# A residual block with shared and routed experts in fp32: second-stage sums kept in PSUM over a block, both first-stage matrices in one bank, a last unit by tokens

## The chip, the core and the metric

The kernel runs on one core of one Trainium2 chip, in fp32 throughout. The metric is the device time of one execution in microseconds (us). The engines are TensorE (PE, matmuls), VectorE (DVE), ScalarE (ACT), GpSimd (POOL, here the indirect gathers and scatters) and SyncE (SP, which issues most DMAs). Matmul results lie in PSUM, in eight banks of 128 partitions x 512 fp32 numbers.

## What is computed

x has 4 x 1024 tokens of 512 numbers; N = 4096 tokens in all. Two layers follow each other, each with a residual:

```python
ys = cond / sqrt(512);  d = rsqrt((ys * ys) @ (w0 * w0) + eps)
x1 = x + ((x * ys) @ w0) * d                          # layer 0
shared = (silu(x1 @ w1) * (x1 @ w3)) @ w2             # 512 -> 1024 -> 512
s = sigmoid(concat(x1, cond) @ router_W)              # 8 experts
# the two best by s + bias; their gates are s, divided by the sum of both
routed = sum of gate_e * (gelu(x1 @ W1e[e]) @ W2e[e]) # 512 -> 512 -> 512, exact gelu
out = x1 + (shared + routed) / 3
```

## The kernel before, in words

**Blocks, units, slots.** The tokens are cut into NB = 8 blocks of TB = 512. A block's shared expert is done in HU = 4 units (class Shared, L719); unit u takes two 128-wide chunks of the hidden width and all 512 tokens. A routed expert is done in slots (class Slot, L953): 256 gathered rows that belong to one expert. SURE = 32 slots are always there; as many more as the routing needs (two here) run in a tc.Switch on the register `spare` (L1207).

**Order of the work.** Layer 0 for all blocks (to about 140 us); Shared units of blocks 0 to 5 (to 578 us); slots 0 to 31 (to 998); the Switch with slots 32 and 33 (to 1038); Shared units of blocks 6 and 7, "the late units". In the late units DVE also adds the routed rows to the tokens (gather_picks and add_picks, L1082 to L1109), in portions that `pump()` hands out at fixed points. Before them the base rows of blocks 0 to 5 are stored to DRAM, and come back as `sum` for this addition.

**Seven products.** Nearly every matrix product is done on 2 x 2 quarters with seven products and sums of quarters (the Winograd form). LO and HI are the first and the last 256 columns. In a Shared unit the *first stage* computes x1 @ w1 (matrix i = 0, the gate) and x1 @ w3 (i = 1, the value). Product n of matrix i is four instructions of 256 columns. Products 1, 6, 5, 3 add up in one chain, whose value between them is copied out by ACT (evict, L773 to L776); 2, 7 and 4 are added to those copies by DVE (add, L778 to L780). Products 6, 5 and 3 need sums of weights, which weight_sums (L418 to L427) makes on DVE for the units of block 0, one unit ahead, a task for each matrix; and sums of tokens (token_sums, L402 to L412).

The *second stage* of a unit, h @ w2, runs one unit later: `rest(prev, task)` (L782) weaves four parts of the unit before (seconds, L846) between its own products. A part's products go to three PSUM banks, a chain and two others (sa, sb, sc in the profile), and its drain (L871 to L881) multiplies by 1/3 and adds to the block's base rows on DVE, seven times a unit. hidden_sums (L830 to L837) makes the sums of h that the second stage needs. Block 0 uses plain matmuls there (plain, L890), with 512 columns and four banks that add up over the block. After the block's last unit `store` writes the base rows out.

**PSUM.** Two pools, bank_a and bank_b, of four banks each in rotation (L95 to L99). A unit takes four bank_a tiles: chain and other, each for both matrices, with half of `chain` unused.

**Order set by hand.** `tasks` (L1151 to L1175) maps a half unit to the small works done at its end: fetches of expert weights on SP's queue (fetch_first, L916, four DMAs of 256 KB from W1e; fetch_second, L922, one of 1 MB from W2e), the router's steps (sigmoid, picks, counting), the sums. In a slot, `rest` issues fetch_first(j + 3) (L996) and, while it runs the parts of the slot before, fetch_second of that slot's j + 3 (L1074). All these fetches stand in SP's queue in the order in which they are issued, among the stores and loads of base rows; ACT's queue carries the stores of the slots' results (ys_d). The main loop is L1204 to L1231.

Of the kernel before, what the change touches and what calls it, by code (L numbers as in the profile page):

```python
# [25 lines left out]
FP = mybir.dt.float32  # L26
# [18 lines left out]
def kernel(  # L45
# [46 lines left out]
    ps_a = ctx.enter_context(tc.tile_pool(name="ps_a", bufs=4, space=bass.MemoryType.PSUM))  # L92
    ps_b = ctx.enter_context(tc.tile_pool(name="ps_b", bufs=4, space=bass.MemoryType.PSUM))

    def bank_a(name):  # L95
        return ps_a.tile([P, TB], FP, tag="a", name=name)

    def bank_b(name):
        return ps_b.tile([P, TB], FP, tag="b", name=name)  # L99

# [407 lines left out]
    def open_pools():  # L508
        lin_ctx.close()
        later["row"] = ctx.enter_context(tc.tile_pool(name="row", bufs=6))  # L510
        sums = ctx.enter_context(tc.tile_pool(name="sums", bufs=1))
        hs = sums.tile([P, 3 * TH], FP, name="hs")
        more = sums.tile([P, 3 * TH], FP, name="more")
        later["hs"] = [hs[:, ts(n, TH)] for n in range(3)]
        later["more"] = [more[:, ts(n, TH)] for n in range(3)] + [falling.rearrange("p t e -> p (t e)")]
        work = ctx.enter_context(tc.tile_pool(name="work", bufs=1))
        t_tiles.append(work.tile([P, 3 * KH * TH], FP, name="t1"))
        later["g"] = work.tile([P, 2 * TB], FP, name="g")
        later["h"] = [work.tile([P, 2 * TB], FP, name=f"h{i}") for i in range(2)]
        rt = rt_ctx.enter_context(tc.tile_pool(name="rt", bufs=1))  # L520
        for name in ("sel", "hit", "one", "two"):
            later[name] = rt.tile([P, NT, E], FP, name=name)
        for name in ("picked", "run"):
            later[name] = rt.tile([P, E, NT], FP, name=name)
        for name in ("top", "den", "live", "half"):
            later[name] = rt.tile([P, NT], FP, name=name)
        for name in ("cnt", "shift", "ns", "upto"):
            later[name] = rt.tile([P, E], FP, name=name)
        later["last"] = rt.tile([P, E + 1], FP, name="last")
        later["full"] = rt.tile([P, E, N // GS], FP, name="full")  # L530
        later["edge"] = rt.tile([P, N // GS], FP, name="edge")
        later["own"] = rt.tile([P, NSLOT, E], FP, name="own")
        later["ownf"] = rt.tile([P, NSLOT], FP, name="ownf")
        later["high"] = [rt.tile([P, NT], I32, name=f"high{i}") for i in range(2)]
        later["low"] = [rt.tile([P, NT], I32, name=f"low{i}") for i in range(2)]
        later["addr"] = addr
        later["toks_raw"] = toks_raw
# [181 lines left out]
    class Shared:  # L719


        py = {}

        def __init__(self, blk, u):
            self.blk, self.u = blk, u
            self.seven = False

        def product(self, out, i, n, start):
# [19 lines left out]
            for k in range(KH):  # L748
# [7 lines left out]
                )  # L756

        def begin(self):

            blk, u = self.blk, self.u  # L760
            self.chain = [bank_a(f"ch{i}_{blk}_{u}") for i in range(2)]
            self.other = [bank_a(f"ot{i}_{blk}_{u}") for i in range(2)]
            for i in range(2):
                self.product(self.chain[i][:, LO], i, 1, True)
            for i in range(2):
                self.product(self.other[i][:, LO], i, 2, True)

        def sevens(self):
            for i in range(2):
                self.product(self.other[i][:, HI], i, 7, True)  # L770
            self.seven = True

        def evict(self, m, cols):  # L773

            for c, p in zip(self.c, self.chain):
                nc.scalar.activation(c[:, m, cols], p[:, LO], AF.Copy)  # L776

        def add(self, half, m, cols):  # L778
            for c, p in zip(self.c, self.other):
                nc.vector.tensor_tensor(c[:, m, cols], p[:, half], c[:, m, cols], ALU.add)  # L780

        def rest(self, prev, task):  # L782
            g, h = self.c = [t.rearrange("p (m t) -> p m t", m=2) for t in (later["g"], later["h"][self.at % 2])]
            self.h = h
            none = (lambda: None, lambda: None)
            parts = prev.parts() if prev is not None else [none] * 4
            self.evict(0, LO)
            for i in range(2):
                self.product(self.chain[i][:, LO], i, 6, False)
                if not self.seven:  # L790
                    self.product(self.other[i][:, HI], i, 7, True)
            self.add(LO, 0, LO)
            pump()
# [3 lines left out]
            drain()  # L797
            for i in range(2):
                self.product(self.chain[i][:, LO], i, 5, False)
            self.evict(1, HI)  # L800
            mm, drain = parts[1]
            mm()
            self.add(HI, 1, HI)
            drain()
            pump()
            for i in range(2):
                self.product(self.chain[i][:, LO], i, 3, False)
            nc.scalar.activation(g[:, 0, HI], self.chain[0][:, LO], AF.Silu)
            nc.scalar.activation(g[:, 0, LO], g[:, 0, LO], AF.Silu)
            mm, drain = parts[2]  # L810
            mm()
            nc.vector.tensor_tensor(h[:, 0, HI], g[:, 0, HI], self.chain[1][:, LO], ALU.mult)
            nc.vector.tensor_tensor(h[:, 0, LO], g[:, 0, LO], h[:, 0, LO], ALU.mult)
            drain()
            task(2 * self.at)
            pump()
            for i in range(2):
                self.product(self.other[i][:, HI], i, 4, False)
            mm, drain = parts[3]
            mm()  # L820
            self.add(HI, 1, LO)
            nc.scalar.activation(g[:, 1, :], g[:, 1, :], AF.Silu)
            drain()
            nc.vector.tensor_tensor(h[:, 1, :], g[:, 1, :], h[:, 1, :], ALU.mult)
            if self.blk > 0:
                self.hidden_sums()
# [18 lines left out]

        def seconds(self, part):  # L846
            blk, u, h = self.blk, self.u, self.h
            if part == 0:
                self.bank2 = [bank_b(f"s{n}_{blk}_{u}").rearrange("p (s d) -> p s d", s=2) for n in "abc"]
            chain, two, seven = self.bank2  # L850
            a11, a12, a21, a22 = h[:, 0, LO], h[:, 1, LO], h[:, 0, HI], h[:, 1, HI]
# [3 lines left out]
            for out, a, b, start in (  # L855
                [(chain, a11, b1[:, LO], True), (two, a12, b2[:, LO], True)],
                [(seven, a21, b1[:, HI], True), (chain, s2, t2, False)],
                [(chain, s1, t1, False)],
                [(chain, s4, b2[:, HI], False), (seven, a22, t4, False)],
            )[part]:  # L860
# [10 lines left out]
        def drain(self, part):  # L871
            blk = self.blk
            chain, two, seven = self.bank2
            for bank, m, half in (
                [(chain, 0, LO), (two, 0, LO)],
                [(seven, 1, HI), (chain, 1, LO)],
                [(chain, 1, HI)],
                [(chain, 0, HI), (seven, 1, LO)],
            )[part]:
                r = base[blk][m][:, :, half]  # L880
                nc.vector.scalar_tensor_tensor(r, bank, third, r, ALU.mult, ALU.add)  # L881
            if part == 3 and self.u == HU - 1:
                self.store()

        def store(self):
# [4 lines left out]
        def plain(self, m):  # L890
            blk, u = self.blk, self.u
            hc = 2 * u + m
            if hc == 0:
                self.py[blk] = [bank_b(f"ps{blk}_{s}") for s in range(NS)]
            for s in range(NS):
# [57 lines left out]
    class Slot:  # L953
# [26 lines left out]
        def rest(self, prev, task):  # L980
# [14 lines left out]
            parts[3]()  # L995
            if self.j + 3 < self.end:  # L996
                fetch_first(self.j + 3)
# [69 lines left out]
        def part3(self):  # L1067
# [5 lines left out]
            nc.scalar.dma_start(out=as_pair(ys_d, j * GS), in_=self.pair)  # L1073
            if j + 3 < self.end:  # L1074
                fetch_second(j + 3)
# [46 lines left out]
    def reload_last():  # L1122
        load_segments(nc.sync, later["segs"][:, : TB // Q, :], x1_d[ts(last_blk, TB)])

    def spare_pair(i):
        return later["segs"].rearrange("p q c -> p (q c)")[:, ts(i, 2 * D)].rearrange("p (s d) -> p s d", s=2)
# [24 lines left out]
    for u, work in (  # L1151
# [12 lines left out]
        (10 * HU + 4, [lambda: turn_rows(0)]),  # L1164
        (2 * early * HU, [lambda: fetch_second(1), lambda: fetch_second(2)]),
        (2 * late, [reload_last, lambda: out_sums(0, big[5])]),
        (2 * late + 1, [lambda: out_sums(1, big[5])]),
        (2 * late + 3, [lambda: out_sums(2, big[5])]),
        (2 * late + 2, [turn_last]),
        (2 * late + 5, [lambda: token_sums(last_blk)]),  # L1170
    ):
        tasks[u] += work
# [32 lines left out]
    for u, unit in enumerate(units):  # L1205
        if u == late:
            for n in tc.Switch(later["spare"], E):  # L1207
                prev.end = SURE + n
                last = prev
                for j in range(SURE, SURE + n):  # L1210
                    slot = Slot(j)
# [16 lines left out]
        prev = unit  # L1228
    for mm, drain in prev.parts():
        mm()  # L1230
        drain()  # L1231

# [38 lines left out]
```

## Time and profile before

| | us |
|---|---|
| median of 4 runs | 1197.2 (1196.25 to 1200.44) |
| the profiled execution | 1200.9 |
| its span | 1199.1 |
| layer 0 | 0 to 139.8 |
| Shared blocks 0 to 5 | 139.8 to 577.9 |
| slots 0 to 31 | 577.9 to 997.8 |
| Switch, slots 32 and 33 | 997.8 to 1037.6 |
| Shared blocks 6 and 7, end | 1037.6 to 1199.1 |

A profile's line names the line of the kernel, the engine, the operation, output and inputs by the program's names, the shape, and in brackets the idle time before it with what ended it. In the first stage `ch` is a chain bank and `ot` the other one; in a slot `ph` is the first stage, `yc` and `yo` the second. Matmul durations overlap a little: four instructions are listed with 1.03 us, but the next four begin 0.86 later.

The page's rows of the evictions and drains that the change touches, with count, busy time, mean ns of one and the idle time before them:

```profile
L776 ACT ACTIVATE g<-ch 128x256 f32<-128x256 f32 x96 | 36.7, 382 | 203.3 <-PE ch L749 191.5
L780 DVE TENSOR_TENSOR g<-ot,g 128x256 f32<-128x256 f32 x96 | 40.3, 420 | 56.8 <-PE ot L749 37.3
L881 DVE SCALAR_TENSOR_TENSOR base<-sa,base 128x512 f32<-128x512 f32 x88 | 60.7, 690 | 19.8 <-PE sa L862 18.9
...
L978 ACT ACTIVATE h<-ph 128x512 f32<-128x512 f32 x68 | 40.6, 597 | 156.3 <-PE ph L970 156.3
```

The first two have a twin for h; the third has some with other outputs. The last is a slot's eviction, with twice the columns of the first.

### The profile page before, as it was taken

Reading aid. Unit: us, or ns where it says so; the run is one execution under the profiler, and the core shown is the slowest. Engines: PE = TensorE matmul, PEld = TensorE weight load, DVE = VectorE, ACT = ScalarE, POOL = GpSimd, SP = SyncE. Lnnn points to the kernel's source line nnn. Section 1 sums busy time; section 2 is a strip of 40 time slices with the busy share of each in tenths; the row PEclk is TensorE's granted clock in tenths of the full one; section 3 lists DMA queues with packets and bytes.
Section 4 is the critical chain, followed back from the end, with each engine's and each line's share of the span. In section 5 each row is a group of like instructions: output and inputs, shape, how many; then the busy total and the mean of one; then the engine's idle time right before and its main releaser. Section 6 shows DMA issues by size and latency. Waiting matters only on the chain.

```text
span 1199.1 us, 15347 instructions
## 1 busy us (share of the span) xinstructions
PE 1169.2 (98%) x5138; PEld 957.9 (80%) x5138; DVE 710.9 (59%) x1569; ACT 224.7 (19%) x515; POOL 449.3 (37%) x448
## 2 busy tenths in 40 slices
PE   8999999999999999999989999999999998999997
PEld 5444576788888888888878888888888887787886
DVE  4547555666565655655644554554555554389897
ACT  2000031111221221211111222212212211221120
POOL 3000000344430112202356666676666760056640
PEclk9999999999999999999999999999999999999999
DMA  9599410210502016140297898888988885487861
GB/s 170 106 223 206 92 50 1 84 23 1 71 1 76 27 36 184 53 123 17 81 264 226 236 262 229 239 254 235 246 255 242 235 252 160 117 266 246 298 211 71
DMA packets 120153, 184.97 MB, mean 154 GB/s; under 512 B 13797, under 2 KB 48741, under 8 KB 120057
## 3 DMA queue, kind: packets, MB, share of 16 engines
q1 hardware_dynamic: 85944, 123.92, 39.7%
q0 software_dynamic: 16448, 35.26, 10.4%
q10 hardware_dynamic: 17664, 24.65, 6.3%
q8 instruction: 43, 0.70, 0.3%
q14 instruction: 54, 0.43, 0.2%
HBM read 139.14 MB, written 44.64 MB: 153 GB/s over the span
## 4 chain that ended last, share of the span: by engine, by line
PE 85%; DVE 6%; DMA 5%; issue 2%; SPq 1%; ACTq 0%; ACT 0%; DVEq 0%
PE ph L970 19%; PE ch L749 16%; PE ot L749 12%; PE yc L1028 10%; PE yo L1028 7%; PE sa L862 7%; PE pl L443 6%; PE sc L862 3%; PE ps L896 2%; DMA seg<-in_x_dram 2%; PE sb L862 2%; DMA big<-in_L_cond_W2e_dram 1%; DVE sum L1107 1%; DVE xsegs L881 1%; SPq L122 1%
## 5 line engine op out<-in xcount | busy, mean ns | idle before, releaser
L939 POOL DMA_INDIRECT xsegs<-x_d,toks x280 | 306.4, 1094 | 320.0 <-DVE xg L951 79.0
L654 POOL DMA_INDIRECT tok_d<-token,addr x64 | 64.7, 1010 | 287.2 <-DVE addr L644 272.2
L1041 DVE TENSOR_TENSOR yr<-yo,yr 128x256 f32<-128x256 f32 x102 | 43.3, 425 | 187.1 <-ACT yr L1038 95.3
L970 PE MATMUL ph<-xg,big 128*128 128x256 f32 x544 | 130.2, 383 | 4.7 <-DMA big<-in_L_cond_W2e_dram 4.7
L970 PE MATMUL ph<-t,big 128*128 128x256 f32 x544 | 128.5, 379 | 0.0
L443 PE MATMUL pl<-xT,wm 128*128 128x512 f32 (+1 forms) x288 | 117.4, 554 | 3.5 <-DVE xT L282 1.5
L970 PEld LDWEIGHTS ph<-xg,big 128*128 128x128 f32 x544 | 104.4, 192 | 19.5 <-issue 5.0
L970 PEld LDWEIGHTS ph<-t,big 128*128 128x128 f32 x544 | 103.4, 190 | 14.1
L749 PE MATMUL ot<-big,w_sb 128*128 128x256 f32 x448 | 110.4, 379 | 0.1
L1096 POOL DMA_INDIRECT big<-ys_d,addr x64 | 68.7, 1074 | 101.8 <-DMA xsegs<-x_d 56.7
L443 PEld LDWEIGHTS pl<-xT,wm 128*128 128x128 f32 x288 | 52.4, 190 | 55.3 <-issue 46.3
L749 PEld LDWEIGHTS ot<-big,w_sb 128*128 128x128 f32 x448 | 85.0, 190 | 12.8 <-issue 0.8
L1038 ACT ACTIVATE yr<-yc 128x256 f32<-128x256 f32 x136 | 52.1, 383 | 210.4 <-PE yc L1028 201.9
L776 ACT ACTIVATE g<-ch 128x256 f32<-128x256 f32 x96 | 36.7, 382 | 203.3 <-PE ch L749 191.5
L780 DVE TENSOR_TENSOR g<-ot,g 128x256 f32<-128x256 f32 x96 | 40.3, 420 | 56.8 <-PE ot L749 37.3
L881 DVE SCALAR_TENSOR_TENSOR base<-sa,base 128x512 f32<-128x512 f32 x88 | 60.7, 690 | 19.8 <-PE sa L862 18.9
L780 DVE TENSOR_TENSOR h<-ot,h 128x256 f32<-128x256 f32 x96 | 40.5, 422 | 50.7 <-PE ot L749 38.9
L1028 PE MATMUL yc<-w0t,g 128*128 128x256 f32 x272 | 69.9, 379 | 0.5 <-ACT yr L1038 0.5
L978 ACT ACTIVATE h<-ph 128x512 f32<-128x512 f32 x68 | 40.6, 597 | 156.3 <-PE ph L970 156.3
L749 PE MATMUL ch<-w0t,seg 128*128 128x256 f32 x256 | 62.6, 380 | 2.5 <-issue 2.5
L749 PE MATMUL ch<-t,seg 128*128 128x256 f32 x256 | 63.1, 379 | 0.0
L1028 PEld LDWEIGHTS yc<-w0t,g 128*128 128x128 f32 x272 | 51.6, 190 | 7.8 <-ACT yr L1038 0.9
(222 smaller groups left out, 1882.4 us busy)
## 6 DMA issues: line engine op xcount, KB each, us to landing
big<-in_L_cond_W1e_dram SPq DMA_DIRECT2D x140, 256.0 KB, 5.4
big<-in_L_cond_W2e_dram SPq DMA_DIRECT2D x34, 1024.0 KB, 7.8
ys_d<-yr ACTq DMA_DIRECT2D x34, 512.0 KB, 8.7
x_d<-back SPq DMA_DIRECT2D x32, 256.0 KB, 5.0
base<-x_d SPq DMA_DIRECT2D x13, 512.0 KB, 4.5
base_d<-base SPq DMA_DIRECT2D x12, 512.0 KB, 4.3
sum<-base_d SPq DMA_DIRECT2D x12, 512.0 KB, 7.1
out_dram<-sum SPq DMA_DIRECT2D x12, 512.0 KB, 4.5
```

Of the source, the lines that this page charges most:

```text
L443: nc.tensor.matmul(pas[oc][:, ds(lo, n)], lhsT=wms[b][:, k, oc, :], rhs=xTs[blk][:, k, ds(lo, n)], start=(k == 0), stop=(k == KC - 1),)
L654: ins = nc.gpsimd.indirect_dma_start(out=tok_d, out_offset=bass.IndirectOffsetOnAxis(ap=later["addr"][i][:, t : t + 1].bitcast(U32), axis= ...
L749: nc.tensor.matmul(out, lhsT=lhs[:, k, :], rhs=rhs[:, k, :], start=start and k == 0, stop=k == KH - 1, skip_group_check=not start,)
L780: nc.vector.tensor_tensor(c[:, m, cols], p[:, half], c[:, m, cols], ALU.add)
L862: nc.tensor.matmul(out[:, s], lhsT=a[:, ts(s, P)], rhs=b, start=start and s == 0, stop=True, skip_group_check=not (start and s == 0),)
L881: nc.vector.scalar_tensor_tensor(r, bank, third, r, ALU.mult, ALU.add)
L939: nc.gpsimd.indirect_dma_start(out=seg[:, q, :], out_offset=None, in_=x1_segs, in_offset=bass.IndirectOffsetOnAxis(ap=toks[:, c : c + 1].b ...
L970: nc.tensor.matmul(self.ph[:, i], lhsT=weights[j][0][:, k, ts(c, P)], rhs=xg[j][:, k, :], start=(k == 0), stop=(k == KC - 1),)
L1028: nc.tensor.matmul(out, lhsT=a[:, k, :], rhs=b[:, k, :], start=start and k == 0, stop=k == HC // 2 - 1, skip_group_check=not start,)
L1038: nc.scalar.activation(self.r[r][:, cols], self.chain[:, LO], AF.Copy)
L1041: nc.vector.tensor_tensor(self.r[r][:, cols], self.other[:, half], self.r[r][:, cols], ALU.add)
L1096: nc.gpsimd.indirect_dma_start(out=picks[t][i], out_offset=None, in_=ys_d, in_offset=bass.IndirectOffsetOnAxis(ap=at.bitcast(U32), axis=0) ...
```

## The change

1. *Second stage.* bank_b has four fixed banks b0 to b3. The products `two`, `seven` and a new `four` add up in b0 to b2 over all units of a block, and are drained only in the unit that `closes` it (u = 3; in block 7 u = 2). The chain has b3 in every unit. Drains go from seven a unit to four, and eight in the closing one.
2. *First stage.* Both matrices share banks: chain, `two` and `seven`, each with two halves of 256 columns, one for each matrix; three bank_a tiles a unit and not four. ACT evicts both halves in one instruction, into g and h that lie beside each other in one tile (hgh = h, g, h), and DVE adds both in one. As h takes turns on the two sides of g, the order of the matrices is (1, 0) in even units and (0, 1) in odd ones. In unit 0 of block 0, whose sevens are there already, the order of products stays; elsewhere both matrices' 6 come before both 7.
3. *Last unit* (block 7, u = 3). Its second stage is done by tokens (finish): eight plain matmuls of 512 columns into four banks, each drained and stored by itself (256 KB, SP and ACT in turn). It needs no hidden sums, but the unchanged half of w2's chunk 6, which a new task reloads (128 KB).
4. *Fetches.* fetch_second(1) is issued one task earlier, at the end of the last unit of block 5, and so ahead of slot 0's fetch_first(3) and the base stores in SP's queue. fetch_first(34) and fetch_second(33) are no longer issued before the Switch but inside its cases, where the case has such a slot. With two spare slots only fetch_second(33) is issued, and fetch_first(34) never is.

```diff
-    ps_b = ctx.enter_context(tc.tile_pool(name="ps_b", bufs=4, ...))
+    ps_b = ctx.enter_context(tc.tile_pool(name="ps_b", bufs=1, ...))
...
+            self.closes = u == (HU - 2 if blk == NB - 1 else HU - 1)
...
+        def pair(self, bank, n, start):
+            for spot, i in enumerate(self.turn):
+                self.product(bank[:, spot], i, n, start and spot == 0)
...
         def begin(self):
-            self.chain = [bank_a(f"ch{i}_{blk}_{u}") for i in range(2)]
-            self.other = [bank_a(f"ot{i}_{blk}_{u}") for i in range(2)]
...
+            self.turn = (1, 0) if self.at % 2 == 0 else (0, 1)
+            self.chain, self.two, self.seven = (
+                bank_a(f"{n}_{name}").rearrange("p (i t) -> p i t", i=2) for n in ("ch", "tw", "se")
+            )
+            self.pair(self.chain, 1, True)
+            self.pair(self.two, 2, True)
...
-            for c, p in zip(self.c, self.chain):
-                nc.scalar.activation(c[:, m, cols], p[:, LO], AF.Copy)
+            nc.scalar.activation(self.both[:, :, m, cols], self.chain, AF.Copy)
...
         def rest(self, prev, task):
...
-            for i in range(2):
-                self.product(self.chain[i][:, LO], i, 6, False)
-                if not self.seven:
-                    self.product(self.other[i][:, HI], i, 7, True)
+            self.pair(self.chain, 6, False)
+            if not self.has_seven:
+                self.sevens()
...
+                chain = bank_b(f"s{blk}_{u}", 3)
+                if u == 0:
+                    self.sums[blk] = [bank_b(f"s{n}_{blk}", n) for n in range(3)]
...
-                [(chain, s4, b2[:, HI], False), (seven, a22, t4, False)],
+                [(chain, s4, b2[:, HI], False), (four, a22, t4, u == 0)],
...
+            each = [(chain, 0, LO)], [(chain, 1, LO)], [(chain, 1, HI)], [(chain, 0, HI)]
+            whole = [(two, 0, LO)], [(seven, 1, HI)], [(seven, 1, LO)], [(four, 1, LO)]
+            for bank, m, half in each[part] + (whole[part] if self.closes else []):
...
+        def finish(self):
+            banks = [bank_a("f0"), bank_b("f1", 0), bank_b("f2", 1), bank_a("f3")]
+            for m in range(2):
+                for s in range(NS):
+                    nc.tensor.matmul(banks[s], lhsT=self.h[:, m, ts(s, P)], rhs=w2_sb[:, 2 * u + m, :], ...)
+            for s in range(NS):
+                r = base[blk][s // 2][:, s % 2]
+                nc.vector.scalar_tensor_tensor(r, banks[s], third, r, ALU.mult, ALU.add)
+                eng = (nc.sync, nc.scalar)[s % 2]
+                eng.dma_start(out=out_f[ds(blk * TB + s * P, P)], in_=r)
...
-            if self.j + 3 < self.end:
+            if self.j + 3 < self.end and self.j != SURE - 1:
                 fetch_first(self.j + 3)
...
-            if j + 3 < self.end:
+            if j + 3 < self.end and j != SURE - 2:
                 fetch_second(j + 3)
...
-        (2 * early * HU, [lambda: fetch_second(1), lambda: fetch_second(2)]),
+        (2 * early * HU - 1, [lambda: fetch_second(1)]),
+        (2 * early * HU, [lambda: fetch_second(2)]),
...
+        (2 * (late + HU + 1), [reload_w2]),
...
             for n in tc.Switch(later["spare"], E):
+                if n > 1:
+                    fetch_second(SURE + 1)
+                if n > 2:
+                    fetch_first(SURE + 2)
...
-    for mm, drain in prev.parts():
-        mm()
-        drain()
+    prev.finish()
```

## The prediction

> **What bounds the kernel now.** I read the page first (its span and busy shares), then the waits of TensorE, then the timeline at every wait. The page:
>
> ```profile
> span 1199.1 us, 15347 instructions
> ...
> PE 1169.2 (98%) x5138; PEld 957.9 (80%) x5138; DVE 710.9 (59%) x1569; ACT 224.7 (19%) x515; POOL 449.3 (37%) x448
> ```
>
> TensorE (PE) is busy in 98% of the span, so time leaves by two doors only: less PE work, or fewer of its 30 idle us. In the middle of blocks 1 to 5 a unit takes 18.12 us (354.26 to 372.39, 84 matmul instructions of 0.2157 us pitch, no gap), and the change leaves these 84 as they are. So I go to the waits (line waited at, releaser, total, times, longest):
>
> ```profile
> PE ph L970 <- DMA big<-in_L_cond_W2e_dram: 4.7, 1, 4.7
> PE yc L1028 <- DMA big<-in_L_cond_W2e_dram: 3.5, 1, 3.5
> PE sa L862 <- DVE base L881: 2.6, 2, 1.4
> PE ch L749 <- issue: 2.5, 1, 2.5
> ...
> PE ot L749 <- DVE g L780: 1.3, 1, 1.3
> ...
> PE yc L1028 <- ACT yr L1038: 0.9, 2, 0.5
> ```
>
> The reader sees two long waits for expert weights, some of 1 to 1.5 us behind VectorE (DVE), and the last row, the price of a bare eviction between two products of one chain: 0.47 each. The timeline at three of these places:
>
> ```profile
> 180.34 0.42 DVE L425 TENSOR_TENSOR seg<-seg,w_sb 128x256 f32<-128x256 f32 x1
> ...
> 180.87 1.10 PE L749 MATMUL ch<-w0t,seg 128*128 128x256 f32 x4 [2.53 <-issue]
> ...
> 609.12 1.39 PE L1028 MATMUL yc<-big,h 128*128 128x256 f32 x4 [3.46 <-DMA big<-in_L_cond_W2e_dram]
> ...
> 1002.48 3.58 PE L970 MATMUL ph<-xg,big 128*128 128x256 f32 x8 [4.66 <-DMA big<-in_L_cond_W2e_dram]
> ...
> 1004.26 0.69 DVE L1021 TENSOR_TENSOR w0t<-big,w0t 128x512 f32<-128x512 f32 x1 [5.98 <-issue]
> ```
>
> "issue" at 180.87 is the weight sum of L425, which ends at 180.76. After the other two, eight matmuls take 3.58 and not 1.73. A table of stretches tells why (third column from the right: granted clock):
>
> ```profile
> 609.80:613.20 3.40, 3.40 (x9) 2.71 (x9) 3.33 (x7) 0.38 (x1) 0.00 (x0) 0.50 1.07 297
> ...
> 1002.30:1005.70 3.40, 3.22 (x8) 2.62 (x9) 1.41 (x3) 0.00 (x0) 0.00 (x0) 0.50 0.98 270
> ```
>
> For 3.4 us after each wait the clock is halved: 1.7 us lost each time. The profiled execution took 1200.9 us, the median of the runs is 1197.2, and one of the four runs (1200.44) lies like the profile. The difference, 3.7, is about twice 1.7, so I take it that the common run has no such halving, and sum twice.
>
> **What the change adds.**
>
> 1. *Unit 0 of block 0 and unit 0 of block 6.* Here no unit before fills the gaps. Today one matrix is evicted (0.38 us, L776) beneath the product of the other; 16 matmuls run unbroken from 147.05 and from 1044.57. With both in one bank, the next pair waits until 128x512 elements are out. In the Switch's last slot the same sequence has one product of 0.86 every 1.50 us (1032.65, 1034.15): 0.64 lost per eviction of 0.38. The L978 eviction of 128x512 takes 0.60, so 0.64 + 0.21 = 0.86, at products 5 and 3: 2 x 2 x 0.86 = **+3.4**. From 2.6 (0.64 each) to 3.4.
>
> 2. *Unit 2.* Its order of matrices becomes (1, 0), so its product 6 begins with matrix 1, whose sums are the last of a DVE queue (pick_second, count, then L424 to L427). Today 6 and 7 of matrix 0 run first (176.45 to 178.17) and PE loses 180.87 - 178.17 = 2.70. After, PE stands from 176.45, and DVE arrives later as well: the sigmoid and the picks stand behind the silu of L808, which waits for the pair (+0.86), and one 0.69 add for two matrices holds back the first by 0.28: 1.15. Lost 180.87 + 1.15 - 176.45 = 5.57; more by **+2.9** (1.7 if DVE is not late).
>
> 3. *Unit 3.* Product 6 of matrix 1 moves from 200.34 to 199.48, and its sum (L425, ends 199.31) comes about 0.85 late: 200.16 + 0.05. **+0.7** (0 to 0.7).
>
> 4. *All other units.* The eviction of 0.60 lies beneath the other bank's pair or prev's parts (1.73 each; it needs 0.86). The tight place is at the end: silu waits for both matrices, so the drain of (chain, 1, HI) ends about 357.99 and not 357.74, and PE wants that bank at 358.58 (part 3). At least 0.3 us stay: 0. ACT's and DVE's fewer instructions buy nothing there either, as PE has no gap.
>
> What the skill says of it: the page "PSUM — Partial Sum Buffer", section "PSUM bank collisions raise a hardware error", wants PSUM guarded by bank and quadrant, not by address. That rule speaks against the shared bank, for it lets nobody evict one half while the other is written. No run here shows a collision. By the rule every shared bank costs what item 1 counts; by row 1034.15 only where nothing lies between.
>
> **What it removes.**
>
> 5. *W2e for slot 1.* SP issues it third today, behind two base stores and the four W1e transfers of slot 3 (593.5), at 596.60; it lands 12.4 us later, DVE's L1016 waits 7.73, PE 3.46, and slot 2 takes 18.35 us, not 12.95. After, it is issued when PE leaves block 5's x1T, about 576.3, 33 us before its use. On SP it passes fetch_first(3) and the stores, which are due only at 590: nobody waits behind it. W2e for slot 2 takes the old place, landing near 609 for a use near 614. **-3.7** without a halved clock, -5.4 with it.
>
> 6. *The Switch.* The wait list blames W2e for the 4.66, but DVE, which has no such transfer to wait for, stands 5.98 at "issue", and PE's loads 5.03. So it is mostly the branch itself. W1e for slot 34 (1 MB, never used here) goes, and the DMA share of 1.03 falls with it. From 0 to all (-6.3 with the clock); nearest the "issue" row: **-0.8**. W2e(33) is now issued inside the case; its DVE use is a slot (12.95) away, its landing 7.8 by the page: hidden. Fetch_first(34) is never issued.
>
> 7. *Late units* (blocks 6 and 7, add_picks on DVE). Unit lengths exceed 18.12 by 5.95 in all: 21.4, 19.6, 18.73, 18.72. DVE is busy 135.65 of 161.5 us there. It loses 16 drains of 56 at 0.60 pitch, an add per pair (0.16 x 3 per unit) and four hidden sums: about 13 us. The 1.33 at 1072.83 goes for sure (product 2 takes another bank); the rest lessens, but add_picks stays. From -1.33 to -5.95; the middle: **-3.6**.
>
> 8. *The last unit.* Its last first-stage pair ends at 1182.59 and the span 16.5 later, with four waits. After: part 3 of unit 2 (8 x 0.216 = 1.73), eight 512-column matmuls (L896: eight instructions in 3.43, 16 here: 6.86), 0.21 to the drain, 0.69: 1192.1. The second half of h is ready at 1185.8, wanted at 1187.8. Then a store; the end today is 4.43 after the last drain: 1196.5. **-2.6** (to -4.2 with the 2.8 us of an xsegs store).
>
> reload_w2 (128 KB) and the ACT queue's two stores lie beside all this.
>
> **Sum.** Without halved clocks: +3.4 + 2.9 + 0.7 - 3.7 - 0.8 - 3.6 - 2.6 = -3.7, from the median: **1193.5**. For a profiled run with them: item 5 gives 1.7 more, item 6 0.8, and item 2's idle of 5.6 us takes perhaps 1.2: -5.0, so 1195.9.
>
> The page "TensorE: Matmul & The Clock Gate", Part 1, tells of a free-running window of about 3.4 us: an idle window halves the clock. The trace agrees (halved after 3.46 and 4.66, not after 2.53). By that rule item 2's new 5.6 us are likely to cost 1.7 more in most runs, and the sum would be 1195.2.
>
> **Rivals.** A change within 0.3% (3.6 us: 1193.6 to 1200.8) is what this kernel's measurement can't tell from none.
>
> - *More comes free.* All 5.95 of the late stage goes (-2.3 more) and the Switch falls to half of its 4.66 (-1.5 more): **1189.7**. For it: DVE sheds 13 us where 6 are lost. Against: the add_picks chain that DVE alone carries, and the 5.98 at "issue".
> - *It doesn't do what it says.* The Switch keeps its 4.66 (+0.8), and the late waits come back behind add_picks, all but the 1.33 (+2.3): **1196.6**.
> - *Slower: the silu chain.* In about 27 units with a unit before them, the drain before part 3 must come within the 0.3 to 0.6 us left. If the wait for both matrices makes it later than that, each unit pays. From 0.27 us a unit beyond the slack (7.3 / 27) the kernel is slower than 1200.8; at 0.5, +13.5: **1207**. For it: it repeats all through the shared stage, and DVE's tasks (token and output sums) come in that place. Against: 0.25 us is all that the row shows as shift, and DVE has three drains fewer in its way.
>
> **Chances.** The forecast (1191.5 to 1195.5, half of it beneath the bound) 0.42; more comes free 0.22; not what it says 0.18; slower 0.18. Faster 0.21 + 0.22 = 0.43, same 0.21 + 0.18 = 0.39, slower 0.18. The range leaves out the slower case and little else: 1187.5 to 1201.
>
> **What would show it.** Two new gaps of about 0.86 in each of the two first units; unit 2's wait near 5.6 and, behind it, a clock of 0.5 or not; no wait for W2e near 609; the Switch's wait unchanged if it is "issue"; late units near 18.1; four stores ending about 14 us after the last first-stage pair. Wrong it would be above all by a gap of a few tenths in every unit at part 3, or by late waits that return elsewhere.

## The result, and the profile after

The changed kernel takes 1198.7 us in the median (44 runs, 1195.1 to 1204.4), the one before 1197.3 (67 runs). The ratio is 1.0013, with a 95% interval from 1.0006 to 1.0021: slower by 1.6 us. Forecast was 3.7 us faster, so 5.3 us are to be explained. It lies in the range and within the 0.3% that the text took for no change, but on the other side.

The page of the changed kernel has the same span and the same share for TensorE; VectorE lost 53 us and ScalarE 15, which bought nothing:

```profile
span 1199.3 us, 14865 instructions
...
PE 1170.8 (98%) x5126; PEld 956.6 (80%) x5126; DVE 658.1 (55%) x1413; ACT 209.4 (17%) x419; POOL 456.8 (38%) x448
```

The waits of TensorE, as before: line, releaser, total, times, longest.

```profile
PE ch L759 <- issue: 5.4, 1, 5.4
PE ch L759 <- ACT hgh L789: 4.7, 6, 1.2
PE s L877 <- DVE base L893: 4.3, 3, 2.8
PE ph L1001 <- DMA big<-in_L_cond_W1e_dram: 3.4, 1, 3.4
```

The wait for W2e in slot 2 is gone, the one in unit 2 has doubled (2.5 to 5.4), six waits for the shared eviction are new, and the third row holds one of 2.8 that the prediction does not have. The timeline at these places:

```profile
148.60 1.99 PE L759 MATMUL ch<-w0t,seg 128*128 128x256 f32 x8 [0.69 <-ACT hgh L789]
151.28 1.99 PE L759 MATMUL ch<-big,seg 128*128 128x256 f32 x8 [0.69 <-ACT hgh L789]
...
182.79 3.75 PE L759 MATMUL ch<-w0t,seg 128*128 128x256 f32 x8 [5.38 <-issue]
206.17 1.13 PE L759 MATMUL ch<-w0t,seg 128*128 128x256 f32 x4 [0.58 <-DVE seg L431]
254.05 1.13 PE L877 MATMUL s<-big,hs 128*128 128x256 f32 x4 [2.79 <-DVE base L893]
```

Two rows of 0.69 are the eviction of unit 0. The eight matmuls after the 5.38 take 3.75 and not 1.9: the clock is halved there, and not for one stretch of 3.4 us but for two (third column from the right: granted clock; in the second row it is the mean of a halved and a full part):

```profile
182.70:186.20 3.50, 3.41 (x8) 2.82 (x9) 1.26 (x3) 0.00 (x0) 0.00 (x0) 0.50 0.02 5
186.20:189.60 3.40, 3.40 (x14) 2.88 (x14) 0.00 (x0) 0.60 (x1) 0.00 (x0) 0.82 0.00 0
```

By the trace's clock record the halving runs from 180.63, still inside the wait, to 187.46; the 4.7 us of work under it lose 2.3. At 254.05 TensorE waits for a drain, and the drain waits for the rows it adds to:

```profile
253.30 0.69 DVE L893 SCALAR_TENSOR_TENSOR base<-s,base 128x512 f32<-128x512 f32 x1 [7.53 <-DMA base<-x_d]
```

To see what each place is worth I took, for every Shared unit, the time from its first product to the next unit's first product, and the same for the slots. Units and slots that are not in the table have 18.12 and 12.95 (18.95 in block 0; slots 32 and 33 with the end of the Switch 14.7 and 20.5) in both kernels.

| place | forecast | before | after | difference | other traces of the same place |
|---|---|---|---|---|---|
| unit 0 of block 0 | +1.7 | 14.25 | 16.16 | +1.9 | 16.16 to 16.17 |
| unit 2 | +2.9 | 22.08 | 27.24 | +5.2 | 26.7 to 27.8 |
| unit 3 | +0.7 | 19.04 | 19.88 | +0.8 | 19.88 |
| second unit of block 1 | 0 | 18.46 | 21.19 | +2.7 | 19.2 to 20.5 |
| slot 2 | -3.7 | 18.34 | 12.95 | -5.4 | before: 14.5 to 15.2 |
| last sure slot and Switch entry | -0.8 | 17.78 | 16.52 | -1.3 | before: 16.7 to 18.2, after: 15.5 to 16.5 |
| first late unit | +1.7 | 13.89 | 16.85 | +3.0 | 16.5 to 16.8 |
| other late units but the last | -3.6 | 114.7 | 112.6 | -2.1 | 112.6 |
| start of the last unit to the end | -2.6 | 32.9 | 29.3 | -3.6 | 29.3 |

Layer 0, which the change leaves alone, adds -1.1 (it takes 138.5 to 140.1 us in the traces of all runs). The differences sum to +0.2, as the two spans have it (1199.1 and 1199.3).

### The profile page after: what moved, and what is told of

It is laid out like the page before. It is cut to its first block, busy times and chain, and to the rows that moved or that the text cites. A ratio compares the mean times of both kernels' runs of the same rounds, so it can differ in the third digit from the quotient of the medians.

```text
span 1199.3 us, 14865 instructions
## 1 busy us (share of the span) xinstructions
PE 1170.8 (98%) x5126; PEld 956.6 (80%) x5126; DVE 658.1 (55%) x1413; ACT 209.4 (17%) x419; POOL 456.8 (38%) x448
## 4 chain that ended last, share of the span: by engine, by line
PE 88%; DMA 6%; DVE 3%; SPq 1%; issue 1%; ACT 1%; ACTq 0%; POOL 0%; DVEq 0%; POOLq 0%
PE ph L1001 19%; PE ch L759 17%; PE s L877 13%; PE yc L1059 10%; PE se L759 8%; PE yo L1059 7%; PE pl L449 6%; PE tw L759 4%; PE ps L927 2%; DMA seg<-in_x_dram 2%; DMA ys_d<-yr 1%; DMA base<-x_d 1%; DMA w0t<-in_L_cond_weight_dram 1%; PE f L903 1%; PE pq L378 0%
## 5 line engine op out<-in xcount | busy, mean ns | idle before, releaser
L893 DVE SCALAR_TENSOR_TENSOR base<-s,base 128x512 f32<-128x512 f32 x111 | 75.3, 688 | 82.6 <-PE s L877 75.1
L1001 PEld LDWEIGHTS ph<-xg,big 128*128 128x128 f32 x544 | 103.4, 190 | 17.8 <-issue 3.8
L789 ACT ACTIVATE hgh<-ch 128x512 f32<-128x512 f32 x96 | 57.2, 596 | 280.1 <-PE ch L759 264.8
L793 DVE TENSOR_TENSOR hgh<-se,hgh 128x512 f32<-128x512 f32 x64 | 44.1, 689 | 86.4 <-ACT hgh L789 75.9
L877 PE MATMUL s<-w_sb,hgh 128*128 128x256 f32 x324 | 78.7, 379 | 0.0
L1059 PE MATMUL yc<-big,hgh 128*128 128x256 f32 x272 | 70.8, 383 | 0.5 <-ACT yr L1069 0.5
L1059 PE MATMUL yc<-w0t,hgh 128*128 128x256 f32 x272 | 69.9, 379 | 0.5 <-ACT yr L1069 0.5
L877 PEld LDWEIGHTS s<-w_sb,hgh 128*128 128x128 f32 x324 | 61.6, 190 | 8.4
L1009 ACT ACTIVATE hgh<-ph 128x512 f32<-128x512 f32 x68 | 40.6, 597 | 155.5 <-PE ph L1001 155.5
L1059 PE MATMUL yo<-big,hgh 128*128 128x256 f32 x272 | 64.6, 380 | 0.0
L759 PEld LDWEIGHTS ch<-w0t,seg 128*128 128x128 f32 x256 | 49.2, 194 | 18.3 <-issue 5.8
```

What stands on the lines that cost most here:

```text
L759: nc.tensor.matmul(out, lhsT=lhs[:, k, :], rhs=rhs[:, k, :], start=start and k == 0, stop=k == KH - 1, skip_group_check=not start,)
L789: nc.scalar.activation(self.both[:, :, m, cols], self.chain, AF.Copy)
L793: nc.vector.tensor_tensor(r, bank, r, ALU.add)
L877: nc.tensor.matmul(out[:, s], lhsT=a[:, ts(s, P)], rhs=b, start=start and s == 0, stop=True, skip_group_check=not (start and s == 0),)
L1001: nc.tensor.matmul(self.ph[:, i], lhsT=weights[j][0][:, k, ts(c, P)], rhs=xg[j][:, k, :], start=(k == 0), stop=(k == KC - 1),)
L1059: nc.tensor.matmul(out, lhsT=a[:, k, :], rhs=b[:, k, :], start=start and k == 0, stop=k == HC // 2 - 1, skip_group_check=not start,)
```

## The experiments

Names: a_ stands for the changed kernel with an edit, b_ for the kernel before with one, and c_ has edits of both kinds. Each but b_again, which is one execution, was timed against the kernel before on the same chip; the ratios are to that.

**a_again.** No edit.

> The changed kernel once more, for a second trace and a second comparison. Theory (sum of places): unit lengths show again 16.2 for unit 0 (14.25 before), about 27 for unit 2 (22.1), about 21 for the second unit of block 1 (18.5), 16.9 for the first late unit (13.9), and 12.95 for slot 2 (18.3); time within 2 us of 1198.7. Rival (the wait of 2.79 us for block 1's base rows is a chance of one execution, from transfers that happened to be slow): that unit shows about 18.3 this time, and the rest as above.

Measured: 1197.5, ratio 1.0002 (0.9986 to 1.0018). Unit 2 takes 26.7, unit 0 16.16, the first late unit 16.8. The wait for block 1's base rows is there again, with 1.78; it is no chance of one execution.

**a_sums.**
```diff
-            tasks[2 * u - 2 + i].append(lambda u=u, i=i: weight_sums(u, (i,)))
+            tasks[2 * u - 2 + i].insert(0, lambda u=u, i=i: weight_sums(u, (i,)))
```

> The changed kernel with the weight sums put ahead of the router's steps among the tasks of a half unit. Theory: the wait of 5.4 us in unit 2 and the half clock after it (together 8.2 us in a unit that takes 19.0 without) go, and nothing else on DVE is late: 1198.7 - 8 = about 1190.5, ratio to before about 0.994. Rival: the router's steps, 1.7 us later, make a later unit wait (the counting matmuls of the next unit, or weight sums of unit 3), and only half of it is won: about 1194.5.

Measured: 1190.9, ratio 0.9933 (0.991 to 0.9956): 6.6 us below a_again by the medians (8.3 by the two ratios). Unit 2 now takes 19.3 and unit 3 19.0, and TensorE runs through. The timeline of its unit 2:

```profile
176.33 1.89 PE L759 MATMUL tw<-big,w_sb 128*128 128x256 f32 x8
178.05 1.89 PE L759 MATMUL ch<-w0t,seg 128*128 128x256 f32 x8
179.78 1.89 PE L759 MATMUL se<-big,w_sb 128*128 128x256 f32 x8
```

Product 6 starts at 178.05, straight after product 2. The router's steps, now 1.7 us later, keep nobody waiting. The rival falls.

**a_apart.**
```diff
+            self.lone = self.at in (0, late)
+            banks = [bank_a(f"{n}_{name}") for n in (("ch", "ci", "tw", "se") if self.lone else ("ch", "tw", "se"))]
+            self.chain = banks[:2] if self.lone else banks[0].rearrange("p (i t) -> p i t", i=2)
...
+            if self.lone:
+                for spot in range(2):
+                    nc.scalar.activation(self.both[:, spot, m, cols], self.chain[spot][:, LO], AF.Copy)
```

> The changed kernel, but in the two units with no unit before them (the first of block 0 and the first of block 6) the two chains have a bank each and are evicted one by one. Theory: the gaps of 0.69 us between products 6, 5 and 3 go; unit 0 falls from 16.2 to about 14.3, the first late unit from 16.9 to about 14.6 (its 0.74 behind ACT may stay): 1198.7 - 4.2 = 1194.5. Rival (the gap is the eviction's latency and not its sharing, 0.47 with the short one as in the Switch's last slot): unit 0 falls by 0.4 only, 1197.9.

Measured: 1194.2, ratio 0.9974 (0.9958 to 0.999): 3.3 below a_again. Unit 0 is back at 14.26, the first late unit at 14.47 (13.9 before the change; kernels with part 4 and without shared banks have 14.4 to 14.6, see item 1 below). Its unit 0, a product of each matrix in turn and no gap:

```profile
146.74 1.03 PE L759 MATMUL ci<-w0t,seg 128*128 128x256 f32 x4
147.60 1.03 PE L759 MATMUL ch<-w0t,seg 128*128 128x256 f32 x4
148.46 1.03 PE L759 MATMUL ci<-w0t,seg 128*128 128x256 f32 x4
149.33 1.03 PE L759 MATMUL ch<-big,seg 128*128 128x256 f32 x4
```

It was the sharing of the bank, not the latency of an eviction.

**a_base.**
```diff
-        tasks[2 * blk * HU].append(lambda blk=blk: fetch_pairs(blk))
+        tasks[2 * blk * HU - 4 * (blk == 1)].append(lambda blk=blk: fetch_pairs(blk))
```

> The changed kernel with the load of block 1's base rows two units earlier, so that it stands ahead of the store of block 0 in SP's queue. Theory: the wait of 2.79 us for these rows in the second unit of block 1 belongs to the change in most executions; that unit falls from 21.2 to 18.1-18.5 and the kernel to about 1196. Rival (a chance of that execution): the median stays at 1198.7 within 0.7 us.

Measured: 1197.6, ratio 1.0003 (0.9988 to 1.0019), the same as a_again. In the trace the wait is gone: the first drain of block 1 (248.75) waits for TensorE alone, and the unit takes 18.1. But unit 2 took 27.8 in that execution, a microsecond more than in a_again. So the place is cured and the gain, some 2 us by the traces, is not seen in the times; this one stays inconclusive.

**b_again.** The kernel before, one profiled execution.

> The kernel before once more, for a second trace. If the wait for W2e in slot 2 is systematic, slot 2 shows 16.4 to 18.4 us again (12.95 without a wait; 3.5 of wait, and 1.7 to 1.9 more where the clock is halved after it) and the Switch about 4 to 4.7 of wait. If the two halvings were a chance of the first trace, as the prediction took it, the clock stays at 1.00 there and the execution takes about 1197.

Measured: 1195.4 for the profiled execution, 5.5 below the one of the prediction. Slot 2 took 14.53 and not 18.34, as the wait was 1.0 and not 3.5:

```profile
PE ph L970 <- DMA big<-in_L_cond_W1e_dram: 3.6, 1, 3.6
...
PE yc L1028 <- DMA big<-in_L_cond_W2e_dram: 1.0, 1, 1.0
```

Three more kernels with the old order of fetches (b_psum, b_finish and b_shared) had 15.2, 14.5 and 14.7 there. The trace that the prediction read had drawn the longest of five. After the Switch the clock is low here too (0.67 from 996 to 1001), and in all five traces of the old order, so the halving there was no chance of the first trace; the length of the wait in slot 2 was.

**b_fetch.** Part 4 of the change alone on the kernel before (its hunks are in the diff above).

> The kernel before with part 4 of the change alone (fetch_second(1) one task earlier, the last fetches moved into the Switch). Theory: slot 2 falls to 12.95 and the Switch loses about 1 us of its wait: 1197.1 - 5.4 - 1.2 = about 1190.5 with the halved clock, 1192.5 where it was not halved. Rival (the wait returns at another weight): within 1 us of before.

Measured: 1194.1, ratio 0.9974 (0.9957 to 0.999): -3.1, with an interval from -5.1 to -1.2. Slot 2 takes 12.95, the slot before the Switch 16.0, and the first late unit 14.6, which is 0.75 more than before. The first estimate was too high for the reason seen in b_again. The windows of this trace hold something new (clock third from the right):

```profile
178.20:180.90 2.70, 0.53 (x3) 0.51 (x4) 2.57 (x10) 0.00 (x0) 0.00 (x0) 1.00 0.00 0
180.90:184.30 3.40, 3.40 (x10) 2.72 (x9) 0.80 (x3) 0.38 (x1) 0.00 (x0) 0.52 0.00 0
```

The old wait of 2.5 us in unit 2, which left the clock alone in four other traces, here halved it: unit 2 took 23.8 and not 22.1.

**b_fetch_sums.** b_fetch with the edit of a_sums.

> The kernel before with part 4, and with the weight sums ahead of the router's steps (which takes away its wait of 2.53 us in unit 2). Theory: 2.5 to 2.7 below the kernel with part 4 alone, about 1188.5. It has the four banks, 28 drains a block and the old end, so the distance to the changed kernel with all repairs tells what the shared banks, the sums in PSUM and the end by tokens bring together.

Measured: 1190.4, ratio 0.9947 (0.9931 to 0.9963): 3.7 below b_fetch. Unit 2 takes 19.3: the wait of 2.5 was never needed.

**b_psum.** Part 1 alone: fixed banks, sums in PSUM over a block.
```diff
-                [(chain, s4, b2[:, HI], False), (seven, a22, t4, False)],
+                [(chain, s4, b2[:, HI], False), (four, a22, t4, u == 0)],
...
+            for bank, m, half in each[part] + (whole[part] if self.closes else []):
```

> The kernel before with part 1 of the change alone: two, seven and four add up in PSUM over a block, 20 drains a block in place of 28; first stage, end and fetches as before. Theory: DVE is late in the late units only, so only they gain; of the 5.9 us by which they exceed 18.12 some 2 go (the changed kernel, with three drains and a third of the adds less, showed 2.1 less), and the tail, which had one drain of each kind waiting, gains or loses up to 1. Ratio 0.998. Rival (the gain in the late units came from the joint adds of part 2, or from the freed bank): within 0.5 us of before.

Measured: 1194.5, ratio 0.9983 (0.997 to 0.9996): -2.0. The late units fall to 20.75, 19.15, 18.72 and 18.29 (21.38, 19.62, 18.72, 18.72 before): -1.5 in all; the last unit ends 32.2 us after its start and not 32.9. The rival falls by the places: the late units gain without the joint adds. But part 2 alone takes 1.3 off the same units (b_shared), so either part brings most of the 2.1 of the whole change, and the two overlap.

**b_finish.** Part 3 alone.
```diff
-    for mm, drain in prev.parts():
-        mm()
-        drain()
+    prev.finish()
```

> The kernel before with part 3 alone: the last unit's second stage by tokens. Theory: the span ends 29.3 us after the last unit begins and not 32.9, all else as before: -3.6, about 1193.6, ratio 0.997. Rival (the gain there came from DVE's fewer drains in the unit before, which this kernel does not have): -2.0 or less.

Measured: 1193.8, ratio 0.9977 (0.9967 to 0.9987): -2.8; the span ends 29.4 us after the last unit's start, where it was 32.9. The last drains come every 0.86 us, as the banks fill, and wait for nothing else:

```profile
1186.98 0.69 DVE L899 SCALAR_TENSOR_TENSOR xsegs<-f,xsegs 128x512 f32<-128x512 f32 x1 [0.17 <-PE f L890]
1187.84 0.69 DVE L899 SCALAR_TENSOR_TENSOR xsegs<-f,xsegs 128x512 f32<-128x512 f32 x1 [0.17 <-PE f L890]
```

**b_shared.** Part 2 alone: the first stage of the changed kernel; second stage, end and fetches as before.

> The kernel before with part 2 of the change alone: both first-stage matrices in one bank, evicted and added together, order (1, 0) in even units. Theory (it alone carries the loss, and only at its places): unit 0 +1.9, unit 2 +4.7 to +5.7 with the halved clock, unit 3 +0.8, the second unit of block 1 +1 to +2.7, the first late unit +2.6, late units 0 to -1: +10 to +12, about 1208, ratio 1.009. This is also what is left when the measured ratios of the parts (0.9983, 0.9977, 0.9974) are taken from that of the whole change (1.0013): +0.8%. Rival (the parts do not add up, and the loss is made by the sums in PSUM and the shared banks together): under 1.006.

Measured: 1210.2 where the kernel before took 1201.1 in the same series, ratio 1.0055 (1.0029 to 1.0082). (The kernel before spread from 1197.6 to 1209.6 there, so the medians lie further apart than the ratio; the means are 1209.8 and 1202.8.) The places: unit 0 16.17, unit 2 26.8, unit 3 19.88, the first late unit 16.1, late units 1.3 less in all: +8.5 by the traces, which lies within the interval, but its middle (+6.6) lies under the bound that the theory gave, and 1.0055 is just under the 1.006 that stood for the rival. The time alone does not part the two; the places do, as the loss stands where the theory has it, in a kernel without the sums in PSUM. This trace also has 4.8 us of waits in slots 15, 28 and 29, which no other trace has. The four parts' ratios multiply to 0.9989, with an uncertainty that takes in the 1.0013 of the whole change. The second unit of block 1 took 18.65 here and 18.46 in b_psum (18.45 before): the long wait for the base rows appears with neither part alone, only in kernels with both.

**c_all.** Parts 1, 3 and 4, with the edits of a_sums and a_base, and without part 2.

> Parts 1, 3 and 4 of the change with the weight sums first and block 1's base rows early, and without part 2 (each matrix has its own banks and evictions, as before). The kernel with all repairs, which has part 2 and two banks in the first units, took 1185.3. Theory: part 2 is worth nothing by itself but DVE's and ACT's shorter adds and evictions in the late units: 0 to 1.5 us slower than that kernel, 1185.3 to 1186.8. Rival one (the shared banks carry the late units' gain): 1187.5 or more, with late units of 21.4 and 19.6 again. Rival two (they cost something in every unit): faster than 1184.5.

Measured: 1186.0, ratio 0.9913 (0.9898 to 0.9928), as the theory has it. The late units take 20.75 and 19.15, so the first rival falls; the second falls by the time. Unit 0 takes 14.26 and unit 2 19.3.

**a_best.** The changed kernel with the edits of a_sums, a_apart and a_base.

> The changed kernel with all three repairs: weight sums first, two chain banks in the units without a predecessor, block 1's base rows early. Theory (the places add up): from 1197.5, -6.6 (sums, measured), -3.3 (banks, measured), -1.5 (base rows, by the traces): about 1186, ratio 0.991. Rival (they cover each other, as DVE is later or earlier): not under 1188.5.

Measured: 1185.3, ratio 0.9904 (0.9879 to 0.9929), 1.0% under the kernel before. The repairs add up. The 5.4 and the wait for block 1's base rows are gone (the third row below is the two waits of 0.75 in the late units), and of the six waits for an eviction one of 1.2 and one of 0.3 are left. The largest that remain:

```profile
PE ph L1011 <- DMA big<-in_L_cond_W1e_dram: 3.1, 1, 3.1
PE se L759 <- DVE x1T L413: 1.5, 1, 1.5
PE s L887 <- DVE base L903: 1.5, 2, 0.8
```

Against c_all nothing can be told apart (0.9904 and 0.9913, with intervals wider than the difference). So the shared banks, once repaired, bring nothing that these runs can measure, though they halve the number of adds and evictions.

## Why the prediction was wrong

It named eight places, and seven of them moved the way it said. Its sum failed by sizes, and by one place that it did not have.

- *Item 2 and the two sums: the step that cost most.* The cause (product 6 of matrix 1 stands behind the router's steps, and VectorE comes later) and the wait were right: 5.57 forecast, 5.54 measured by the same count (5.38 as the trace lists the gap); VectorE was 1.14 late by the trace, 1.15 in the text. What failed is "I take it that the common run has no such halving": the sum for the median left the halved clock out of item 2. All five traces with this wait show it, and unit 2 cost +5.2 and not +2.9: the missing 2.3 are the halved clock. The paragraph on the clock had it with +1.7 and the sum did not take it; and 1.7 is one stretch of 3.4 us, where all five traces have two (6.83 us, 1.8 to 2.9 lost). The reading came from the 3.7 us between the profiled execution and the median, which was put down to two halvings. In b_again, 5.5 us faster, most of the difference is slot 2 (3.8), whose wait for W2e was 1.0 and not 3.5.
- *Item 5.* -3.7 was read from one trace with a long wait. Five traces of the old order lose 5.4, 1.6, 2.3, 1.5 and 1.7 there. Items 5 and 6 together, forecast -4.5, gave -3.1 (b_fetch). (The eight matmuls in 3.58 are those after the Switch alone; slot 2's row has four in 1.39.)
- *Item 4, "all other units: 0".* The silu chain is as forecast, and a shared bank costs nothing where other products lie between: units stand at 18.12. But the first unit that adds to block 1's rows waits for them, 0.8 to 2.8 us in four traces. The six transfers (two stores, four loads) go out right behind block 0's last drains. Before the change the first drain found its rows there, 8.7 us after the load was issued; after it, the first load lands 11.8 to 12.7 us after issue (in the two traces of the changed kernel), and SP needs 3 us and not 2 to issue the two stores. The text priced SP's queue only where the diff moved something. Why the same six transfers are slower when parts 1 and 2 come together is open; neither part alone shows it.
- *Item 1.* Unit 0 was near (+1.9 for +1.7). In the first late unit the loss was +3.0 and not +1.7. Part 2 alone made 2.2 of it (b_shared: 16.1); the other 0.75 belongs to part 4 and not to the shared bank. ScalarE's first eviction starts 6.1 us after its last instruction in the Switch, where it was 3.7, and TensorE waits for it, 0.74. This parts the traces cleanly: 5.8 to 6.1 in all nine traces of kernels with part 4, 3.7 in the five of kernels without. Three of the nine have no shared banks, and TensorE waits there too, as in b_fetch:

```profile
1039.30 1.99 PE L749 MATMUL ch<-w0t,seg 128*128 128x256 f32 x8 [0.51 <-ACT g L776]
```

The text priced only what part 4 saves at the Switch. Why ScalarE comes later when the fetches stand inside the cases is open.
- *Item 6.* Right in kind: W2e(33) is issued at 1006.77 in the changed kernel, after TensorE resumed at 1005.37, so the remaining 3.4 us cannot be a wait for it. -1.1 to -1.3 for a forecast of -0.8.
- *Item 7.* The middle of the bounds (-3.6) was too much; -2.1. Two waits of 0.75 and one of 1.24 stay. The 1.33 at product 2, which went "for sure", came back in the same unit as 1.24 at product 6. The same unit in a_best's trace tells why (rows between left out):

```profile
1059.81 2.94 DVE L1148 SCALAR_TENSOR_TENSOR xsegs<-big,gate,xsegs 128x512 f32<-128x512 f32 x4
...
1062.79 0.68 DVE L800 TENSOR_TENSOR hgh<-se,hgh 128x512 f32<-128x512 f32 x1
...
1063.51 0.63 ACT L843 ACTIVATE hgh<-hgh 128x512 f32<-128x512 f32 x1 [7.11 <-DVE hgh L800]
1064.04 0.58 ACT L796 ACTIVATE hgh<-ch 128x512 f32<-128x512 f32 x1
...
1064.68 1.99 PE L759 MATMUL ch<-w0t,seg 128*128 128x256 f32 x8 [1.23 <-ACT hgh L796]
```

VectorE adds four picks in a row; the add of product 4 stands behind them, ScalarE's silu waits for that add, and the eviction that TensorE needs stands behind the silu. Fewer drains do not help where a whole portion of picks stands ahead.
- *Item 8.* -3.6 for -2.6. To the last drain the gain is the 2.6 of the text; but the end comes 3.4 us after that drain, and the text had kept the old 4.4. The stores of 256 KB land in 2.0 to 2.1 us.

In numbers, against the forecast of -3.7: unit 2 +2.3, base rows +2.7, late units +1.5, units 0 and 3 +0.3, part 2 in the first late unit +0.5, the end -1.0, and of part 4 +1.4, by b_fetch (its 0.75 in the first late unit is in that). That is +7.7, and would make +4.0 where +1.6 is measured. Single traces scatter by some microseconds, and the base rows' share is not confirmed by the times (a_base); how the 2.4 divide among the places is not settled.

Of the rivals, none came about. The slower one had the right sign, and it was the wrong mechanism: nothing is lost in each unit, all in five places.

## What to carry to other kernels

- When an engine is busy in 98% of a span, a change that saves work on the others has no place to pay; what it does to the few waits decides, and there the order in a queue (the sums behind the router's steps) was worth more than all instructions saved. One moved line (a_sums) gave 6.6 us, where the whole change had lost 1.6.
- Two buffers joined into one also join what waits for them. Look for the stretches without other work to hide the longer release: the first unit, the first after a branch.
- Read a wait for a transfer from more than one trace, or take its low end; and price a clock drop into every new gap that can fill most of a stretch of 3.41 us, and not only into one longer than that.

## What the runs showed of the hardware

The half clock does not follow a gap by its length. After 5.4 us in unit 2 it came in five traces of five, after 2.5 us in one of five (b_fetch: 0.52 for the next 3.4 us). After 3.41 us at the Switch it came in the changed kernel; after 3.42 us there it did not in a_apart.

The clock records of the traces show what it does follow. Within each trace every halving begins a whole number of 3.413 us after the one before it: in the first trace at 609.80 and at 1002.33, which is 115 times that. So I cut each trace into windows of 3.413 us on this raster and took TensorE's idle share in each. In the 14 traces, up to TensorE's last product, the half clock followed every window at full clock that was idle for 63% or more (18 of them), and none that was idle for 54% or less. In b_fetch the 2.5 us lay in one window, which was idle for 74%; in the other four traces a boundary cut the gap, and no window was idle for more than 53%. The 3.42 us of a_apart were cut into 47% and 53%. The prediction's reading (halved after 3.46 and 4.66, not after 2.53) held for its trace because of where the gaps lay. The full clock came back after a halved window with at most 4% of idle time, and not after one with 21% or more: so the 5.4 us halve two windows, and unit 2 varies from 26.7 to 27.8 with the work that falls under them.

The Trainium skill, page "TensorE: Matmul & The Clock Gate", Part 1, has a free-running window of about 3.4 us that must be idle. The raster agrees with the window. That it must be idle does not agree if it means idle throughout, since 63% was enough; here the measurement decides.

The same transfers differ between executions more than I had expected: a wait of 3.5 or of 1.0 for the same 1 MB, and 16.7 to 17.8 us for the same slot before the Switch. A Shared unit that waits for no transfer and meets no halved clock repeats within a few hundredths.
